# A graph network's layers 1 and 2: one full product per block in place of quarter-array products for two, and a sum over chunks by VectorE ahead of the sum over nodes

## The chip, the cores and the metric

The kernel runs on one core of one Trainium2 chip. The metric is the device time of one execution in microseconds; the time before is the median of three runs.

## What is computed

Four graph layers follow each other over `x` of 8 batches, 2048 nodes and 64 features. Each layer takes a layer norm and a relu of `x` and adds its result to `x`. The two layers that the change touches, and the last one that the sum over nodes belongs to, are these:

```python
# layer 1, three steps: v <- relu([v, A v] W1^T + b1) W2^T + b2
for _ in range(3):
    effects = einsum('nm,bmd->bnd', adj, v)
    h = concatenate([v, effects], -1)
    h = relu(einsum('bnk,dk->bnd', h, W1) + b1)
    v = einsum('bnk,dk->bnd', h, W2) + b2
x = x + v

# layer 2: one aggregation, a scale and bias for each feature, a linear map
h = maximum(layernorm(x), 0)
agg = einsum('ij,bjf->bif', adj, h)
x = x + einsum('bnf,of->bno', (agg*c*w_nl[:,0] + agg*c*w_nl[:,1] + b_nl), w_out) + b_out

# layer 3: attention over adj > 0.5
h = maximum(layernorm(x), 0)
x = x + elu(softmax(where(adj > 0.5, leaky(s1 + s2^T), -9e15)) @ h)
```

No entry of the given `adj` is above 0.5, so the attention of layer 3 is the mean of `h` over all nodes. The kernel computes that mean and, beside it, tests that the adjacency has the form that this path needs; a general path behind it runs only if the test fails.

## The kernel before

The 8 batches are taken as 4 pairs. The 2048 nodes of a pair are 4 blocks of 512, each with 4 chunks of 128 nodes. A block lies either with its nodes on the partitions (128 partitions, 4 chunks, 128 columns: 64 features of each of the two batches) or with its features on them (128 x 512).

The product with the adjacency (`product`, line 250) takes 32 matrix products of 128 x 128 by 512 columns for a block: 16 chunks, each as a high and a low part of the values (`H` and `L`). The `fill` dictionary names functions that are called between these products, after chunk number `m`; that is how small products of other blocks are put into the stream. After it `scaled` (line 240, VectorE) multiplies the result with the row factors.

Layer 1 goes over the pairs, three steps and four blocks. In each block the result of the aggregation (`g`) and the mapped old features (W1v times `gT[nb]`) are added (line 917, VectorE), then ScalarE applies bias and relu (918). The mapping is done by `map_two` (895 to 907) after chunk 10 of blocks 0 and 2, for two blocks at once. W1v stands twice on the diagonal of a 128 x 128 matrix, so `map_two` takes only the two 64 x 64 blocks: for two node blocks and two batches these are four products of 64 x 64 by 512 columns, each in another quarter of the TensorE array. They go into a tile of two PSUM banks (tag `big`), and ScalarE copies the four results back over `gT`. `finish` (873) brings a block back to nodes by four products of 128 columns (`bn`, line 665) and makes the new high and low parts. In the last step `prepare_next` loads the next pair's block, transposes it (`pt`, line 262, tag `tr`), multiplies it (`bn_u`) and splits it. Two small copies of a constant row (`hb<-ivt`, line 681) belong to it.

Layer 2 goes over pairs and blocks. After chunk 5 of a block, `behind` continues the norms in work and finishes the block before (`finish2`): four products `bn`, an add, and the start of its norm. The norm (`norm_stages`) has three stages: mean, difference and square; variance and its power on GpSimd (194); and the scaling on VectorE (197), after which `done` is called with the result. After chunk 15, `sums(g - 2)` (957 to 966) adds the nodes of block g - 2 for layer 3: four products with a matrix of ones, one for each chunk, accumulated in one PSUM bank `pS` (tag `tr`) over the pair's four blocks. After the fourth, `outputs` computes the mean's elu and adds it to all four blocks.

PSUM is full: the tags `mm`, `big` and `tr` have two buffers each, of one, two and one bank. A buffer is given out in turn, and its next user waits until the last reader of its previous one has finished. The order on each engine is made from the program's order by a scheduler that may put an instruction that is ready ahead of one that waits; on the chip each engine then keeps its order.

Of the kernel before, what the change touches and what calls it, by code (L numbers as in the profile page):

```python
# [8 lines left out]
F32 = mybir.dt.float32  # L9
# [5 lines left out]
ALU = mybir.AluOpType  # L15
AX = mybir.AxisListType
# [26 lines left out]
def uniform_path(  # L43
# [30 lines left out]
    nc = tc.nc  # L74
    P = 128
    B, N, C = x.shape
    NP = B // 2
    NCH = N // P
    NB = N // 512
# [6 lines left out]
    psums = [pro.enter_context(tc.tile_pool(name="psump", bufs=1, space=bass.MemoryType.PSUM))]  # L86
# [14 lines left out]
    def bank(tag, name):  # L101
        return psums[-1].tile([P, 512], F32, tag=tag, name=name)
# [11 lines left out]
    ones = consts.tile([P, P], F32, name="ones")  # L114
# [19 lines left out]
    def nodes(acc):  # L134

        return acc.rearrange("p j f -> p (j f)").rearrange("p (e j c) -> p j e c", e=2, c=C)

    def load_x(layer, p, nb, queue=nc.sync):
        acc = block("acc", f"acc_{layer}_{p}_{nb}", 2)
        fill_x(acc, layer, p, nb, queue)  # L140
        return acc
# [11 lines left out]
    def load_crow(nb, name, tag="crow"):  # L153
        t = work.tile([P, 512], F32, tag=tag, name=f"crow_{name}", bufs=2)
        nc.sync.dma_start(t, crowD[:, nb * 512:(nb + 1) * 512].to_broadcast([P, 512]))
        return t
# [4 lines left out]
    def split(t):  # L161
        return t.rearrange("p j (b c) -> p j b c", b=2)
# [11 lines left out]
    def norm_stages(xt, name, done, out_):  # L174

        z = block("z", f"z_{name}", 3)
        g = groups(z)
        mean = small.tile([P, 8], F32, name="mean")
        nc.vector.tensor_reduce(each(mean), nodes(xt), axis=AX.X, op=ALU.add)
        nc.vector.tensor_scalar(mean, mean, 1.0 / C, None, op0=ALU.mult)  # L180
        firsts.append(nc.vector.tensor_tensor(  # L181
            split(z), nodes(xt), each(mean)[:, :, :, None].to_broadcast([P, 4, 2, C]),
            op=ALU.subtract
        ))
        sq = block("sq", f"sq_{name}", 1)
        squares.append(nc.scalar.activation(sq, z, AF.Square))  # L186
        yield
        var = small.tile([P, 8], F32, name="var", bufs=3)
        nc.vector.tensor_reduce(var, groups(sq), axis=AX.X, op=ALU.add)  # L189
        variances.append(  # L190
            nc.vector.tensor_scalar(var, var, 1.0 / C, EPS, op0=ALU.mult, op1=ALU.add)  # L191
        )
        rstd = small.tile([P, 8], F32, name="rstd", bufs=3)
        powers.append(nc.gpsimd.tensor_tensor(rstd, var, mhalf, op=ALU.pow))  # L194
        yield
        h = z if out_ is None else out_
        scales.append(nc.vector.scalar_tensor_tensor(  # L197
            groups(h), g, 0.0, rstd[:, :, None].to_broadcast([P, 8, C]), op0=ALU.max, op1=ALU.mult
        ))
        done(h)  # L200
        yield

    def norm_relu(xt, name, done, out_=None):
        n = norm_stages(xt, name, done, out_)
        next(n)
        pending.append([n, 2])
# [16 lines left out]
    lastp = []  # L223
# [52 lines left out]
    def term(k, name):  # L276
        pool = l0t if k == 1 else l0f[0]
        return pool.tile([P, 512], F32, tag=f"t{k}", name=name, bufs=(2, 4, 1)[k])
# [286 lines left out]
    nm = "0_1_3a"  # L565
    tx = work.tile([P, 512], F32, tag="z", name=f"t1T_{nm}", bufs=3)
    ps = bank("b1", f"bv_{nm}")
    for m in range(NCH):
        if m in (2, 7, 12):
            go_back(1 + m // 5)  # L570
        for i in range(2):
            nc.tensor.matmul(
                ps, hls[1][m // 4][i][:, m % 4, :], BT[:, m, 3 * 512:],
                start=(m == 0 and i == 0), stop=(m == NCH - 1 and i == 1),
# [80 lines left out]
    def feat(i, name):  # L655

        if i == 0:
            return term(1, name)
        return lastp[0].tile([P, 512], F32, tag="fm", name=name, bufs=4)

    def back_to_nodes(fT, wmat, name, tag="big"):

        ps = psums[-1].tile([P, 4, 2 * C], F32, tag=tag, name=f"bn_{name}")
        for t in range(4):
            nc.tensor.matmul(ps[:, t, :], fT[:, t * P:(t + 1) * P], wmat, start=True, stop=True)  # L665
        return ps
# [63 lines left out]
    def feat_0(p, q):  # L730
        h = load_h(p, q, f"f0_{p}_{q}", l0q)
        return to_feat(h, term(0, f"t0T_{p}_{q}"), f"0_{p}_{q}")

    first_t0 = []
    for p in range(NP):
# [47 lines left out]
        for nb in range(NB):  # L783
            nm = f"0_{p}_{nb}b"
# [3 lines left out]
                fill={12: lambda: first_t0.append(feat_0(0, 0))} if p + nb == 0 else {},  # L788
                tag="mm" if p + nb else "b0",
# [32 lines left out]
    w1vT, w1eT, w2T, wos, w1v2, w1e2, r1e, rbo = (wl[:, i, :] for i in range(8))  # L822
# [46 lines left out]
    def layer1(n, p):  # L869
        hl, gT = ops[n]  # L870
        steps = 3
        for s in range(steps):
            last = s == steps - 1
            g_new, hl_new = [], []

            def finish(nb):
                nm = f"1_{p}_{s}_{nb}"
                if last:
                    acc = load_x(1, p, nb)
                    pn = back_to_nodes(g_new[nb], w2T, nm)  # L880
                    nc.vector.tensor_tensor(nodes(acc), split(pn), nodes(acc), op=ALU.add)
                    keep(p, nb, acc, f"2_{p}_{nb}", rows4(rbo))
                else:
                    pn = back_to_nodes(g_new[nb], w1e2, nm)
                    nc.vector.tensor_tensor(split(pn), split(pn), rows4(r1e), op=ALU.add)
                    hl_new.append(halves(pn, nm))

            def mid():
                if last:
                    prepare_next(n + 1, 2)  # L890
                else:
                    finish(2)

            def map_two(nb):

                ph = psums[-1].tile([P, 2, 512], F32, tag="big", name=f"ph_1_{p}_{s}_{nb}")
                w = w1v2 if s else w1vT
                two = (slice(0, C), slice(C, P))
                for i in range(2):
                    for bb in range(2):  # L900
                        nc.tensor.matmul(  # L901
                            ph[two[bb ^ i], bb, :], w[two[bb], two[bb]], gT[nb + i][two[bb], :],
                            start=True, stop=True,
                        )
                for i in range(2):
                    for bb in range(2):
                        nc.scalar.copy(gT[nb + i][two[bb], :], ph[two[bb ^ i], bb, :])  # L907

            for nb in range(NB):
                nm = f"1_{p}_{s}_{nb}"  # L910
                crow = load_crow(nb, nm)
                g = feat((s + 1) % 2, f"g_{nm}")
                fill = {8: mid} if nb == 3 else {}
                if nb % 2 == 0:
                    fill[10] = lambda: map_two(nb)
                product(hl, nb, nm, g, crow, fill=fill)
                gadd = nc.vector.tensor_tensor(g, g, gT[nb], op=ALU.add)
                nc.scalar.activation(g, g, AF.Relu, bias=b1s if s else b1c)
                g_new.append(g)
                go_on()  # L920
                if nb in (1, 2):
                    finish(nb - 1)
                    if last:
                        prepare_next(n + 1, nb - 1)
                if s < 2:
                    k = 2 * (8 * p + 4 * s + nb)
                    with tc.issue_after(gadd.ins):
                        test(k)
                        test(k + 1)
            if last:  # L930
                finish(2)
                prepare_next(n + 1, 3)
            if last and n == NP - 1:

                put_off.append(lambda: finish(3))
            else:
                finish(3)
            gT, hl = g_new, hl_new
# [5 lines left out]
    accs, es, zs, pS = [], [], {}, {}  # L944

    def finish2(g):
        p, nb = divmod(g, NB)
        nm = f"acc_2_{p}_{nb}"
        acc = term(1, nm) if p % 2 else feat(1, nm)
        acc = acc.rearrange("p (j f) -> p j f", j=4)  # L950
        accs.append(acc)
        fill_x(acc, 2, p, nb)
        pn = back_to_nodes(es[g], wos, f"2_{p}_{nb}")
        nc.vector.tensor_tensor(nodes(acc), split(pn), nodes(acc), op=ALU.add)
        norm_relu(acc, f"3_{p}_{nb}", lambda h: zs.update({g: h}))

    def sums(g):
        p, nb = divmod(g, NB)
        if nb == 0:
            pS[p] = bank("tr", f"pS_{p}")  # L960
        for t in range(4):
            nc.tensor.matmul(  # L962
                pS[p][:, :2 * C], ones, zs[g][:, t, :],
                start=(nb == 0 and t == 0), stop=(nb == NB - 1 and t == 3),
            )
        if nb == NB - 1:
            outputs(p)
# [649 lines left out]
```

## Time and profile before

| | us |
|---|---|
| median of the runs (1238.1 to 1239.29) | 1239.18 |
| the profiled execution | 1238.1 |
| its span, first to last instruction | 1236.1 |
| products of layers 1 and 2 with the adjacency, H and L (line 250, 1024 each) | 409.7 and 401.3 busy |
| `ph` (line 901, 64*64, 192 records) | 26.1 busy |
| `pS` (line 962, 128 records) | 18.0 busy |
| copies of `map_two` (line 907, ScalarE, 96) | 55.8 busy |

Layer 1 runs from about 628 us to 1064, layer 2 from there to the end. A fp32 product appears as two records in the profile, so the 64 products of `sums` are 128. Busy times of products overlap, since they are pipelined: a record of 512 columns lasts 0.39 us, while the next one begins 0.23 us after it. What a product costs is therefore read from the starts of its neighbours, not from its own duration.

### The profile page before, as it was taken

The numbers are of one execution on the slowest core, as the hardware profiler recorded it, in microseconds if no ns is written. First come the engines' busy times: TensorE is split into PE (matmuls) and PEld (weight loads), VectorE is DVE, ScalarE is ACT, GpSimd is POOL, SyncE is SP. The second block draws the span as 40 slices with busy tenths as digits, with TensorE's granted clock in tenths as the row PEclk, the third lists the DMA queues.
The fourth block names the chain that finished last, engine by engine and source line by source line (L and its number), as shares of the span: only waits on it lengthen the run. The fifth ranks groups of instructions, "written<-read, shape, count | busy, mean of one in ns | idle before, by whom it ended". The sixth has DMA issues, their size and how long they took to land.

```text
span 1236.1 us, 15662 instructions
## 1 busy us (share of the span) xinstructions
PE 1197.7 (97%) x5798; PEld 843.7 (68%) x5798; DVE 744.7 (60%) x1940; ACT 237.0 (19%) x377; POOL 223.5 (18%) x233
## 2 busy tenths in 40 slices
PE   5899999999999999999989999999999999999995
PEld 4675555555675557655557787787877877888884
DVE  5456888777757774477654436444644545566664
ACT  6610001000010000000022233233223223211100
POOL 5410222211131111011110013003101400331211
PEclk9999999999999999999999999999999999999997
DMA  9951334332332233122256526543743563533311
GB/s 355 379 154 47 102 105 115 84 86 77 90 102 73 64 82 85 54 64 64 60 128 126 134 85 156 132 85 123 158 115 92 154 131 92 155 124 112 119 58 40
DMA packets 100985, 140.99 MB, mean 114 GB/s; under 512 B 43772, under 2 KB 58108, under 8 KB 98852
## 3 DMA queue, kind: packets, MB, share of 16 engines
q1 hardware_dynamic: 82820, 80.74, 24.9%
q0 software_dynamic: 11776, 48.15, 12.9%
q10 hardware_dynamic: 6304, 11.01, 2.8%
q8 instruction: 48, 0.79, 0.3%
q14 instruction: 37, 0.30, 0.1%
HBM read 95.03 MB, written 35.66 MB: 106 GB/s over the span
## 4 chain that ended last, share of the span: by engine, by line
PE 92%; DMA 3%; DVE 3%; issue 1%; POOL 1%; ACT 0%; SPq 0%; POOLq 0%; ACTq 0%
PE bv L250 38%; PE y L711 26%; PE bn L665 5%; PE bv_1b L250 2%; PE bv_3b L250 2%; PE bv_2b L250 2%; PE bv_0b L250 2%; PE ph L901 2%; DMA BT<-in_adj_dram 2%; PE bn_u L665 1%; PE bv_0a L250 1%; PE bv_3a L250 1%; PE pt L262 1%; PE bv_2a L250 1%; PE pS L962 1%; PE bv_1a L250 1%
## 5 line engine op out<-in xcount | busy, mean ns | idle before, releaser
L250 PE MATMUL bv<-BT,H 128*128 128x512 f32 x1024 | 409.7, 400 | 0.0
L250 PE MATMUL bv<-BT,L 128*128 128x512 f32 x1024 | 401.3, 392 | 0.0
L250 PEld LDWEIGHTS bv<-BT,H 128*128 128x128 f32 x1024 | 193.0, 188 | 56.6 <-issue 19.5
L250 PEld LDWEIGHTS bv<-BT,L 128*128 128x128 f32 x1024 | 193.0, 188 | 37.0
L720 DVE SCALAR_TENSOR_TENSOR acc<-y,emb,acc 128x128 f32<-128x128 f32 x512 | 176.3, 344 | 65.7 <-PE y L711 65.7
L720 DVE SCALAR_TENSOR_TENSOR odd<-y,emb,odd 128x128 f32<-128x128 f32 x448 | 153.4, 343 | 0.0
L711 PE MATMUL y<-wt,t0T 64*128 64x512 f32 x512 | 143.7, 607 | 2.4 <-DVE odd L720 1.7
L194 POOL TENSOR_TENSOR rstd<-var,mhalf 128x8 f32<-128x8 f32 x64 | 105.7, 1653 | 182.4 <-DVE var L191 181.0
L240 DVE TENSOR_TENSOR g<-bv,crow 128x512 f32<-128x512 f32 x48 | 33.2, 691 | 173.0 <-PE bv L250 173.0
L186 ACT ACTIVATE sq<-z 128x512 f32<-128x512 f32 x64 | 40.4, 631 | 398.0 <-DVE z L181 388.1
L711 PEld LDWEIGHTS y<-wt,t0T 64*128 64x128 f32 x512 | 45.8, 185 | 63.3 <-issue 57.1
L692 POOL TENSOR_TENSOR acc<-acc,b2r 128x512 f32<-128x512 f32 x16 | 22.2, 1389 | 315.7 <-DVE z L181 315.7
L692 POOL TENSOR_TENSOR acc<-acc,wl 128x512 f32<-128x512 f32 x16 | 20.5, 1283 | 295.8 <-DVE z L181 295.8
L711 PE MATMUL y<-wt,t1T 64*128 64x512 f32 x256 | 66.7, 589 | 0.0
L197 DVE SCALAR_TENSOR_TENSOR z<-z,rstd 128x512 f32<-128x512 f32 x64 | 44.7, 703 | 35.2 <-POOL rstd L194 35.2
L665 PEld LDWEIGHTS bn<-wl,g 128*128 128x128 f32 x384 | 49.8, 193 | 7.5 <-issue 3.0
L665 PE MATMUL bn<-wl,g 128*128 128x128 f32 x384 | 51.5, 277 | 2.6 <-issue 2.6
L189 DVE TENSOR_REDUCE var<-sq 128x8 f32<-128x512 f32 x64 | 43.6, 681 | 15.6 <-ACT sq L186 15.6
L846 DVE SCALAR_TENSOR_TENSOR junk<-mt,cols,st 128x512 uint8<-128x512 bf16 x64 | 47.7, 745 | 2.7 <-DMA mt<-MD 2.3
L907 ACT COPY g<-ph 64x512 f32<-64x512 f32 x64 | 37.2, 581 | 49.6 <-PE ph L901 48.8
L711 PEld LDWEIGHTS y<-wt,t1T 64*128 64x128 f32 x256 | 27.1, 187 | 27.8 <-issue 27.8
L181 DVE TENSOR_TENSOR z<-acc,mean 128x512 f32<-128x512 f32 x56 | 38.3, 692 | 6.0 <-DMA hs<-z 4.6
(213 smaller groups left out, 1649.7 us busy)
## 6 DMA issues: line engine op xcount, KB each, us to landing
BT<-in_adj_dram POOLq DMA_DIRECT2D x16, 1024.0 KB, 19.6
crow<-crowD SPq DMA_DIRECT2D x64, 256.0 KB, 3.4
st<-in_adj_dram SPq DMA_DIRECT2D x64, 256.0 KB, 3.5
hs<-z POOLq DMA_DIRECT2D x40, 256.0 KB, 3.1
xs<-acc POOLq DMA_DIRECT2D x32, 256.0 KB, 2.4
MD<-BT POOLq DMA_DIRECT2D x16, 512.0 KB, 5.6
acc<-xs SPq DMA_DIRECT2D x32, 256.0 KB, 3.9
hb<-hs SPq DMA_DIRECT2D x28, 256.0 KB, 3.5
```

What stands on the lines that cost most here:

```text
L181: firsts.append(nc.vector.tensor_tensor(split(z), nodes(xt), each(mean)[:, :, :, None].to_broadcast([P, 4, 2, C]), op=ALU.subtract))
L186: squares.append(nc.scalar.activation(sq, z, AF.Square))
L189: nc.vector.tensor_reduce(var, groups(sq), axis=AX.X, op=ALU.add)
L194: powers.append(nc.gpsimd.tensor_tensor(rstd, var, mhalf, op=ALU.pow))
L197: scales.append(nc.vector.scalar_tensor_tensor(groups(h), g, 0.0, rstd[:, :, None].to_broadcast([P, 8, C]), op0=ALU.max, op1=ALU.mult))
L250: nc.tensor.matmul(ps, hl[m // 4][i][:, m % 4, :], BT[:, m, nb * 512:(nb + 1) * 512], start=(m == 0 and i == 0), stop=(m == NCH - 1 and i ...
L665: nc.tensor.matmul(ps[:, t, :], fT[:, t * P:(t + 1) * P], wmat, start=True, stop=True)
L692: nc.gpsimd.tensor_tensor(nodes(acc), nodes(acc), more, op=ALU.add)
L711: nc.tensor.matmul(y[:, bb, :], terms[k][hs_, ts], wt[hs_, k, dg * 512:(dg + 1) * 512], start=(k == 0), stop=(k == K - 1),)
L720: last = nc.vector.scalar_tensor_tensor(xj, yd, ec, old, op0=ALU.mult, op1=ALU.add)
L846: nc.vector.scalar_tensor_tensor(junk, mt, cols[:, i, :], st, op0=ALU.mult, op1=ALU.not_equal, accum_out=bad[:, i, q:q + 1],)
L907: nc.scalar.copy(gT[nb + i][two[bb], :], ph[two[bb ^ i], bb, :])
```

## The change

In layer 1 `map_two` and its copies go. Each block has one full product of the 128 x 128 matrix with `gT[nb]`, after chunk 12, into a bank `ph` of the tag `tr`, and the add takes it from there.

In layer 2 `done` of the norm calls `add_chunks`. For all blocks but the last of the kernel, VectorE adds the four chunks into a tile `hs4` of 128 x 128, and `sums` multiplies that alone with the ones. The last block keeps its four products.

```diff
-            def map_two(nb):
-                ph = psums[-1].tile([P, 2, 512], F32, tag="big", name=f"ph_1_{p}_{s}_{nb}")
-                w = w1v2 if s else w1vT
-                two = (slice(0, C), slice(C, P))
-                for i in range(2):
-                    for bb in range(2):
-                        nc.tensor.matmul(
-                            ph[two[bb ^ i], bb, :], w[two[bb], two[bb]], gT[nb + i][two[bb], :],
-                            start=True, stop=True,
-                        )
-                for i in range(2):
-                    for bb in range(2):
-                        nc.scalar.copy(gT[nb + i][two[bb], :], ph[two[bb ^ i], bb, :])
-
             for nb in range(NB):
                 nm = f"1_{p}_{s}_{nb}"
                 crow = load_crow(nb, nm)
+                ph = bank("tr", f"ph_{nm}")
                 g = feat((s + 1) % 2, f"g_{nm}")
                 fill = {8: mid} if nb == 3 else {}
-                if nb % 2 == 0:
-                    fill[10] = lambda: map_two(nb)
+                fill[12] = lambda: nc.tensor.matmul(
+                    ph, w1v2 if s else w1vT, gT[nb], start=True, stop=True
+                )
                 product(hl, nb, nm, g, crow, fill=fill)
-                gadd = nc.vector.tensor_tensor(g, g, gT[nb], op=ALU.add)
+                gadd = nc.vector.tensor_tensor(g, ph, g, op=ALU.add)
...
-        norm_relu(acc, f"3_{p}_{nb}", lambda h: zs.update({g: h}))
+        norm_relu(acc, f"3_{p}_{nb}", lambda h: add_chunks(g, h))
+
+    def add_chunks(g, h):
+        zs[g] = [h[:, t, :] for t in range(4)]
+        if g + 1 < NP * NB:
+            hs4 = lastp[0].tile([P, 2 * C], F32, name="hs4", bufs=2)
+            nc.vector.tensor_reduce(hs4, h.rearrange("p t f -> p f t"), axis=AX.X, op=ALU.add)
+            zs[g] = [hs4]
...
-        for t in range(4):
+        for t, z in enumerate(zs[g]):
             nc.tensor.matmul(
-                pS[p][:, :2 * C], ones, zs[g][:, t, :],
-                start=(nb == 0 and t == 0), stop=(nb == NB - 1 and t == 3),
+                pS[p][:, :2 * C], ones, z,
+                start=(nb == 0 and t == 0), stop=(nb == NB - 1 and t == len(zs[g]) - 1),
             )
```

## The prediction, made before the changed kernel was run

> **What bounds the kernel now.** I read the page's head first, then who waits on TensorE in the stages of layers 1 and 2 (from 628 us on), then TensorE's timeline around the products that change, then the last 20 us of all engines.
>
> From the page:
>
> ```profile
> span 1236.1 us, 15662 instructions
> PE 1197.7 (97%) x5798; PEld 843.7 (68%) x5798; DVE 744.7 (60%) x1940; ACT 237.0 (19%) x377; POOL 223.5 (18%) x233
> PEclk9999999999999999999999999999999999999997
> ```
>
> TensorE is busy 97% of the span at full clock. The waits of TensorE from 628 us to the end:
>
> ```profile
> PE pS L962 <- DVE z L197: 5.3, 1, 5.3
> PE bn L665 <- issue: 2.6, 1, 2.6
> PE bn_u L665 <- ACT gT L267: 0.7, 1, 0.7
> ```
>
> In 608 us there are three waits: one in the tail (5.3), one in the first step of layer 1 (2.6), one of 0.7. Everything else is TensorE's own rate, so a product added or removed in these layers counts in full, and work on VectorE or ScalarE only where it makes TensorE wait. So I need three prices: the quarter-array group `ph` of now, the full `ph` that comes, and the group `pS`.
>
> *Price of `map_two`.* A step of layer 1 without waits (from one `ph` to the next of its kind) is this row of the windows:
>
> ```profile
> 785.53:820.75 35.22, 35.22 (x181) 27.78 (x183) 16.42 (x32) 9.66 (x16) 0.00 (x0) 1.00 0.55 120
> ```
>
> It holds 4 block products of 32, 2 calls of `map_two` and 4 groups `bn`. The timeline paces undisturbed products at 0.2267 us (24 of them from 755.26 to 760.70), so 128 take 29.02. A group of four 128-column products costs 0.908: a block of layer 2 repeats every 9.07 us (1106.68 to 1115.76) and has 32 products (7.25) and two such groups, `bn` and `pS`. Then 35.22 - 29.02 - 4 x 0.908 leaves 2.57, or 1.28 for each `map_two`. The timeline of TensorE shows the same at one place:
>
> ```profile
> 785.14 0.39 PE L250 MATMUL bv<-BT,L 128*128 128x512 f32 x1
> 785.46 1.09 PE L901 MATMUL ph<-g,wl 64*64 64x512 f32 x8
> 786.48 0.19 PEld L250 LDWEIGHTS bv<-BT,H 128*128 128x128 f32 x1 [0.81 <-issue]
> 786.48 0.50 PE L250 MATMUL bv<-BT,H 128*128 128x512 f32 x1
> 786.82 0.39 PE L250 MATMUL bv<-BT,L 128*128 128x512 f32 x1
> 787.05 0.40 PE L250 MATMUL bv<-BT,H 128*128 128x512 f32 x1
> ```
>
> From the last product ahead to the third behind is 1.91; three paces of 0.2267 taken off leave 1.23, and the next ten run at 0.23, which makes up the rest. The eight records (each fp32 product has two) lie in one stretch of 1.09: the four quarters do run beside each other. The gap ahead is 0.32 instead of 0.23.
>
> *Price of a full fp32 product of 512 columns amid such a stream.* The kernel has one kind, the bias product `pb`:
>
> ```profile
> 61.60 0.40 PE L479 MATMUL bv_2a<-BT,L 128*128 128x512 f32 x1
> 61.83 1.02 PE L406 MATMUL pb<-bd,embT 128*128 128x512 f32 x2
> 62.28 0.80 PE L479 MATMUL bv_0a<-BT,H 128*128 128x512 f32 x1
> 62.92 0.40 PE L479 MATMUL bv_1a<-BT,H 128*128 128x512 f32 x1
> ...
> 63.38 0.40 PE L479 MATMUL bv_3a<-BT,H 128*128 128x512 f32 x1
> 63.63 1.12 PE L406 MATMUL pb<-bd,embT 128*128 128x512 f32 x2
> 64.19 0.79 PE L479 MATMUL bv_0a<-BT,L 128*128 128x512 f32 x1
> 64.83 0.39 PE L479 MATMUL bv_1a<-BT,L 128*128 128x512 f32 x1
> ```
>
> From 61.60 to 62.92 lie one `pb` and two paces of that stretch (0.233): 1.32 - 0.47 = 0.85. The second: 1.45 - 0.47 = 0.98.
>
> **What the Trainium skill says.** "TensorEngine Tiling (Array Packing)", Key Properties: tiles execute in parallel, but a change of tiling mode drains the engine. The trace agrees: four quarters in 1.09 us, and the wider gap ahead of them; this is the part that a full product does not pay. "FP8 and Floating Point Precision", TensorE Precision Notes: true FP32 takes four passes. Agrees: 0.85 for 512 columns is 3.8 paces of the single-pass stream (0.2267). "VectorE: DVE Perf Modes", the tier table: fp32 `tensor_tensor` has one rate, with or without a PSUM operand, and `tensor_reduce` one rate too. The trace agrees: L917 from SBUF 690 ns, L881 from PSUM 683, reduce L179 685.
>
> **The change part by part.**
>
> 1. *Layer 1, `map_two` goes.* It runs 4 pairs x 3 steps x 2 times, 24 x 1.28 = 30.7 us of TensorE, all on the path.
>
> 2. *Layer 1, one full `ph` for each block comes.* 48 of them. I take 0.88: the first `pb` (0.85, nothing odd around it) and 0.03 for the slightly slower pace that follows every fp32 group in this stream. Sum 42.2. Parts 1 and 2: +11.5. Ends: 0.85 gives +10.1, 0.98 gives +16.3. So the full array does in two products what the quarters did beside each other in 1.28; only the drain is saved.
>
> 3. *ScalarE loses its 96 copies* (L907, 581 ns, 55.8 us). They ran while TensorE went on, and ScalarE is busy 19%: nothing on the path.
>
> 4. *The add reads `ph` from PSUM* instead of SBUF: 683 against 690 ns, nothing. It waits for `ph` as well, which ends some six products before `bv`.
>
> 5. *The `tr` banks.* `ph` takes one of the two `tr` buffers from the third quarter of its block until the add. Behind it in the ring come the transposes `pt` of the third-step `prepare_next`. The one after the last block takes the buffer of that block's `ph`, so it must wait for the add. At the end of the second pair that add ends at 855.44, while the `pt` now starts at 854.24: 1.2 us later. TensorE has products of the next pair ready (ten of them already lie between `pt` and `bn_u`), and `L` of the last block is ready at 859.23 while its use comes about 862.2, so I cost it at nothing. If the order kept TensorE standing at `pt`, it would be 1.2 us in each of three pairs.
>
> 6. *The wait in the first step.* `bn` at 647.77 waits 2.6 us for the relu, and that stands on ScalarE behind a copy of `ivt` (646.75) that waits for a load. By then two new `ph` and one old group less put TensorE 2 x 0.88 - 1.28 = 0.5 later; the load is not moved by that, so the wait shrinks: -0.5.
>
> 7. *Layer 2, one `pS` product instead of four, blocks 0 to 14.* Four cost 0.908, that is 8 records at 0.1106 and 0.02 around them. Two records: 0.24; with a little for a short product among long ones I take 0.26 (ends 0.24 and 0.40). Each saves 0.65. The sums of blocks 0 to 12 lie before the last `bn` that the tail hangs on (block 14's, at 1210.1): 13 x 0.65 = -8.4 (ends -6.6 and -8.7). That of block 13 lies behind it and only makes TensorE wait for VectorE; that of block 14 lies in TensorE's wait of 5.3.
>
> 8. *VectorE's reduce*, 15 times. Nearest row 685 ns; the strided read might cost more, and I bound it by twice that, below by 0.6. A block of layer 2 has 5.8 us of VectorE in 9.07 (75.9 busy in the 117.8 us from 1088.7 to 1206.5), and the block shrinks to 8.42, and `sums` comes some 5 us behind `z`: hidden, except at the end. There the timeline shows VectorE without a gap:
>
> ```profile
> 1217.02 0.69 DVE L197 SCALAR_TENSOR_TENSOR z<-z,rstd 128x512 f32<-128x512 f32 x1 [0.56 <-POOL rstd L194]
> 1217.71 0.69 DVE L954 TENSOR_TENSOR acc<-bn,acc 128x512 f32<-128x512 f32 x1
> 1217.77 0.97 PEld L962 LDWEIGHTS pS<-z,ones 128*128 128x128 f32 x8 [0.29 <-DVE z L197]
> ```
>
> The reduce of block 14 comes between these first two, and the last norm starts 0.7 later: +0.7 (ends 0 if it is put into a later gap, +1.4).
>
> Sum: +11.5 - 0.5 - 8.4 + 0.7 = +3.3 us. The profiled execution took 1238.1 (its span 1236.1 and 2.0 around it), so 1241.4; the median of the runs is 1.1 above it, which gives 1242.5.
>
> **Rivals.**
>
> *A, not slower: the first wait goes.* The order on ScalarE is set anew, and without `map_two`'s copies (ended at 637.9) the `ivt` copy may fall behind the relus instead of ahead. Then 2.6 of wait go, of which 0.5 is counted, and with it the slow stretch behind it: `bn` 1.39 against 0.8 and six products 2.57 against 1.36, 1.8 in all. That is 3.9 more, 1238.6. It decides from the point where the relu of block 0 stands ahead of that copy. Against it: the copy stood far ahead of its data already, and nothing here moves the load. 0.16.
>
> *B: the full `ph` costs 0.98*, as the second `pb` did: 48 x 0.10 = 4.8 more, 1247.3. Against it: that `pb` is one of two, and its weights waited 0.3 us. 0.10.
>
> *C: TensorE stands at `pt`* (part 5), 3 x 1.2 = 3.6 more, 1246.1. For it: ring order demands the wait. Against it: the order already has products of the next pair ahead of waiting ones. 0.09.
>
> That the change might not do what it says I leave out: in layer 1 the weights are block-diagonal, so one full product covers both batches, and in layer 2 the column sums of four added chunks are those of the block.
>
> **How the numbers follow.** The main case has 0.65, its own range 1240 to 1245. With the bounds of parts 2, 7 and 8 and the rivals the range is 1238.5 to 1247.5. A measurement of this kernel tells 0.2%, 2.5 us, from no change. Main case: 0.17 within it, 0.48 slower. A: 0.04 faster, 0.12 within. B and C: slower. Together 0.04, 0.29, 0.67.
>
> **What would show it.** Right: a step of layer 1 takes about 36.2 us instead of 35.22 (2.57 off, 4 x 0.88 on), a block of layer 2 about 8.42 instead of 9.07, TensorE stays gapless, one reduce of 0.7 ahead of the last `acc`. Wrong: `ph` pieces that cost 1.0 or more (B), `pt` with idle time (C), no wait in the first step (A), a block of layer 2 at 9.0, where the short product would not be cheaper.

## The result, and the profile after

The changed kernel takes 1244.68 us in the median (1244.5 to 1245.27, 4 runs), the kernel before beside it 1239.24. The ratio is 1.0042, interval 1.0025 to 1.006: 5.4 us slower, where 3.3 were predicted. The time lies in the predicted range (1238.5 to 1247.5), but two terms of the sum are wrong, and they offset each other. The page of the changed kernel:

```profile
span 1243.5 us, 15171 instructions
PE 1203.4 (97%) x5612; PEld 850.1 (68%) x5612; DVE 758.4 (61%) x1955; ACT 181.6 (15%) x281; POOL 223.8 (18%) x233
```

TensorE is as full as before, with 186 fewer records; ScalarE has lost its 96 copies. The profiled pair differs by 7.4 us of span, more than the medians do, since the one before was the fastest of its runs and this one the slowest. Who waits on TensorE from 628 us on (total, times, longest), in the changed kernel:

```profile
PE pS L957 <- DVE z L197: 5.6, 1, 5.6
PE bn L665 <- DVE e L240: 4.4, 4, 1.9
PE pS L957 <- DVE hs L949: 1.4, 1, 1.4
PE bn_u L665 <- ACT gT L267: 0.7, 1, 0.7
```

The wait of 2.6 us in layer 1's first step is gone, and a new one has come in layer 2: four times TensorE stands before `bn` until VectorE has made `e`. Cut by the starts of TensorE's groups in the two timelines, the 7.4 us lie as follows.

| stretch | before | after | difference |
|---|---|---|---|
| up to the first product of layer 1 | 629.1 | 628.7 | -0.4 |
| layer 1, to the first product of layer 2 | 443.9 | 451.9 | +8.0 |
| layer 2, to `bn` of the last block | 143.5 | 141.7 | -1.8 |
| from there to the end | 19.6 | 21.2 | +1.6 |

*Layer 1.* Two steps in a row, as windows of the changed kernel (limits; length; busy of TensorE, of its weight loads, of VectorE, ScalarE and GpSimd; then the granted clock, the DMA share and GB/s):

```profile
750.31:786.60 36.29, 36.29 (x170) 29.04 (x169) 19.35 (x39) 5.65 (x9) 5.13 (x6) 1.00 0.61 159
786.60:822.88 36.28, 36.28 (x169) 29.04 (x169) 16.41 (x32) 5.02 (x8) 0.00 (x0) 1.00 0.58 117
```

A step has no gap and takes 1.07 us more than the 35.22 of before: 12.8 in twelve steps. What takes 4.4 of that back is seen on ScalarE in the first step. First the timeline of the kernel before, then that of the changed one:

```profile
646.75 0.30 ACT L681 COPY hb<-ivt 1x128 f32<-1x128 f32 x1 [8.83 <-DMA acc<-xs]
646.96 1.33 ACT L918 ACTIVATE g<-g,b1c 128x512 f32<-128x512 f32 x2
```

```profile
639.11 0.72 ACT L905 ACTIVATE g<-g,b1c 128x512 f32<-128x512 f32 x1 [5.84 <-DVE var L191]
645.98 0.30 ACT L681 COPY hb<-ivt 1x128 f32<-1x128 f32 x1 [6.15 <-DMA hb<-hs]
647.23 0.72 ACT L905 ACTIVATE g<-g,b1c 128x512 f32<-128x512 f32 x1 [0.95 <-DVE g L904]
```

Before, the relus of blocks 0 and 1 stood behind a copy that waited for a load. Now block 0's relu stands ahead of that copy, at 639.1, and its `bn` starts at 645.1 without a wait. With the wait of 2.6 went the slow products behind it, 1.8.

*Layer 2.* A block without a wait takes 8.43 us instead of 9.07, as it should. But of 14 such savings, 9.0 us, only 1.8 arrive. VectorE's timeline in the block with the longest interior wait (start, length, operation, idle time before it and what ended it), in the changed kernel:

```profile
1145.06 0.69 DVE L197 SCALAR_TENSOR_TENSOR z<-z,rstd 128x512 f32<-128x512 f32 x1 [1.81 <-POOL rstd L194]
1145.79 1.07 DVE L949 TENSOR_REDUCE hs<-z 128x128 f32<-128x512 f32 x1
1146.78 0.68 DVE L232 TENSOR_TENSOR L<-hb,H 128x512 fp32r<-128x512 f32 x1
1147.38 0.68 DVE L941 TENSOR_TENSOR acc<-bn,acc 128x512 f32<-128x512 f32 x1
...
1151.64 0.69 DVE L232 TENSOR_TENSOR L<-hb,H 128x512 fp32r<-128x512 f32 x1 [1.45 <-ACT H L230]
1152.25 0.68 DVE L189 TENSOR_REDUCE var<-sq 128x8 f32<-128x512 f32 x1
1152.96 0.17 DVE L191 TENSOR_SCALAR var<-var 128x8 f32<-128x8 f32 x1
1153.04 0.69 DVE L240 TENSOR_TENSOR e<-bv,crow 128x512 f32<-128x512 f32 x1
```

The same stretch, same pair and block, before:

```profile
1136.37 0.69 DVE L197 SCALAR_TENSOR_TENSOR z<-z,rstd 128x512 f32<-128x512 f32 x1 [1.21 <-POOL rstd L194]
1137.25 0.69 DVE L232 TENSOR_TENSOR L<-hb,H 128x512 fp32r<-128x512 f32 x1 [0.19 <-ACT H L230]
1138.62 0.69 DVE L954 TENSOR_TENSOR acc<-bn,acc 128x512 f32<-128x512 f32 x1 [0.68 <-PE bn L665]
```

The reduce takes 1.07 us, not 0.69, and lies ahead of everything that follows in its queue. Behind it: `acc`, which begins the next norm; and `L`, whose end frees the buffer for the next load of `hb`. That load leaves at 1147.49, when `L` ends, and `H` on ScalarE waits for it (first line: start and duration of the load, from the chain that ended last):

```profile
1147.49 3.42 DMA hb<-hs
1150.98 0.62 ACT L230 CAST H<-hb 128x512 fp32r<-128x512 f32 x1 [5.25 <-DMA hb<-hs]
1151.51 0.63 ACT L186 ACTIVATE sq<-z 128x512 f32<-128x512 f32 x1
```

The next `L` on VectorE waits for this `H`. Behind `L` stands `var`, which needs `sq`, and behind `var` stands `e`, done at 1153.7. The products for `e` had ended at 1152.0. On TensorE:

```profile
1153.79 1.39 PE L665 MATMUL bn<-wl,e 128*128 128x128 f32 x8 [1.83 <-DVE e L240]
1154.82 0.77 PE L250 MATMUL bv<-BT,H 128*128 128x512 f32 x1
1155.40 0.63 PE L250 MATMUL bv<-BT,L 128*128 128x512 f32 x1
1155.82 0.63 PE L250 MATMUL bv<-BT,H 128*128 128x512 f32 x1
```

After 1.83 us of wait the next six products begin at 0.43 us from each other instead of 0.23. That block takes 10.16 us instead of 8.43. So 7.1 of the saving are lost (14 x 0.64 = 8.96 saved, 1.82 arrived): 4.4 in the four waits, 1.7 in the slow products, the rest in small pieces. One of the fourteen savings, block 13's, the prediction had not counted itself.

How near the limit this was can be read from VectorE's own waits in layer 2 of the kernel before:

```profile
DVE acc L954 <- PE bn L665: 15.4, 10, 2.6
```

VectorE stood before `acc` until TensorE had made `bn`, in ten of the sixteen blocks, and not evenly: from the block whose `acc` starts at 1130.6 on, four blocks in a row wait 0, 0.7, 1.3 and 2.6 us, the next four 0, 0.7, 2.1 and 2.6. That is 4.5 to 5.3 for four blocks, 1.1 to 1.3 a block: the slack. A faster block takes 0.64 of it and the reduce 1.06, together 1.7: in the changed kernel this wait has shrunk to 0.9 in all, and TensorE waits instead. The reduce's own reader is not what waits: no `pS` before the tail stands for `hs`.

### The profile page after: what moved, and what is told of

Read it like the earlier page. It is cut to its first block, busy times and chain, and to the rows that moved or that the text cites. A ratio compares the mean times of both kernels' runs of the same rounds, so it can differ in the third digit from the quotient of the medians.

```text
span 1243.5 us, 15171 instructions
## 1 busy us (share of the span) xinstructions
PE 1203.4 (97%) x5612; PEld 850.1 (68%) x5612; DVE 758.4 (61%) x1955; ACT 181.6 (15%) x281; POOL 223.8 (18%) x233
## 4 chain that ended last, share of the span: by engine, by line
PE 86%; DVE 6%; DMA 3%; POOL 2%; issue 1%; ACT 1%; POOLq 0%; ACTq 0%; DVEq 0%
PE bv L250 33%; PE y L711 26%; PE bn L665 4%; PE ph L900 3%; DMA BT<-in_adj_dram 3%; PE bv_3b L250 2%; PE bv_2b L250 2%; PE bv_1b L250 2%; PE bv_0b L250 2%; POOL rstd L194 1%; PE bn_u L665 1%; PE bv_0a L250 1%; PE bv_3a L250 1%; PE pt L262 1%; PE bv_2a L250 1%
## 5 line engine op out<-in xcount | busy, mean ns | idle before, releaser
L250 PE MATMUL bv<-BT,H 128*128 128x512 f32 x1024 | 427.5, 417 | 0.0
L250 PEld LDWEIGHTS bv<-BT,L 128*128 128x128 f32 x1024 | 193.3, 189 | 47.9 <-issue 11.5
L905 ACT ACTIVATE g<-g,b1s 128x512 f32<-128x512 f32 x32 | 23.2, 724 | 137.1 <-DVE g L904 137.1
L691 POOL DMA_DIRECT2D hs<-z x32 | 18.6, 582 | 133.5 <-DVE z L197 96.9
```

The source lines that it names most:

```text
L250: nc.tensor.matmul(ps, hl[m // 4][i][:, m % 4, :], BT[:, m, nb * 512:(nb + 1) * 512], start=(m == 0 and i == 0), stop=(m == NCH - 1 and i ...
```

## The experiments

All differences in us are the ratio's share of the median of the kernel before on the same chip (1238.4 to 1238.9); for the kernels with one execution they are plain differences to that median. Each half of the change was run alone, with the other half as before; the edit is then the one half of the diff shown above.

**Layer 1 alone.**

> The change of layer 1 alone, layer 2 as before. Theory 1 (what the two traces suggest): a step of layer 1 takes 1.07 us more, 12.8 us in twelve steps, and the wait of 2.6 us in the first step with the slow products behind it (together 4.4) is gone, because the relu of block 0 now stands ahead of the copy of ivt on ScalarE: 8.4 us slower than before. Rival (as predicted: the wait only shrinks by 0.5): 11 to 12 us slower, with a wait of about 2 us at the first bn.

1246.01 us, ratio 1.0063 (1.0049 to 1.0078), 7.8 us slower (6.1 to 9.7), where theory 1 had 8.4 and the rival 11 to 12. Theory 1 holds: `bn` of block 0 at 646.5 does not wait.

**Layer 2 alone.**

> The change of layer 2 alone, layer 1 as before (quarter-array products). Theory 1: as in the changed kernel, new waits of TensorE for e and for the sum over chunks eat most of what the short sums save: within 2 us of before. Rival (as predicted: all but the last block's reduce is hidden): 7 to 8 us faster, and the waits seen in the changed kernel come from the shifted start of layer 2, not from the reduce.

1236.14 us, ratio 0.998 (0.9973 to 0.9987), 2.5 us faster, a little more than theory 1's 2. The rival, which is the prediction's figure, falls: with layer 1 as before the waits are there too, so they do not come from the shifted start. TensorE's waits in layer 2:

```profile
PE bn L665 <- DVE e L240: 4.1, 5, 2.0
PE pS L970 <- DVE hs L962: 1.8, 1, 1.8
```

The halves add: +7.8 - 2.5 = +5.3, where the whole change measured +5.4. In the traces, from the first product of layer 1 to the end, they are +7.8 and -1.9, and the whole change is +7.8: the long wait with the slow products behind it is not in the trace of layer 2 alone, where no wait before the tail is longer than 0.9. These are single executions, and the medians do not show that difference.

**Layer 2 without the reduce.** This edit and the two further edits of the reduce are shown against the kernel with layer 2 changed alone.

```diff
-            nc.vector.tensor_reduce(hs4, h.rearrange("p t f -> p f t"), axis=AX.X, op=ALU.add)
-            zs[g] = [hs4]
+            zs[g] = [h[:, 0, :]]
```

> As the kernel with the change of layer 2 alone, but the reduce is left out and the sum over nodes takes the first chunk only, so three quarters of the nodes are missing from the mean. Theory 1 (the reduce's 1.06 us on VectorE delays what stands behind it there: the low parts, so the next load, so e): 8 to 9 us faster than before, blocks of layer 2 at 8.43 us without waits. Rival 2 (TensorE, being faster, runs into the loads and the norm chain whatever VectorE does): 2 to 4 us faster, the waits for e remain.

1230.72 us, ratio 0.993 (0.9915 to 0.9945), 8.7 us faster. From the second block to the last but one each takes 8.44 us, and `e` is waited for once, at the end:

```profile
PE bn L665 <- DVE e L240: 0.6, 1, 0.6
```

From block 0's `bn` to block 14's it takes 8.2 us less than before (4.7 less with the reduce), and from there to the end 26.0, as before (29.0 with the reduce). So TensorE's saving was there to be had, and it was the reduce that took it.

**The reduce replaced.** GpSimd adds in two steps; then VectorE in two plain adds.

```diff
-            nc.vector.tensor_reduce(hs4, h.rearrange("p t f -> p f t"), axis=AX.X, op=ALU.add)
+            nc.gpsimd.tensor_tensor(h[:, 0:2, :], h[:, 0:2, :], h[:, 2:4, :], op=ALU.add)
+            nc.gpsimd.tensor_tensor(hs4, h[:, 0, :], h[:, 1, :], op=ALU.add)
```

> The change of layer 2 alone, but GpSimd adds the chunks (two adds, of 256 and of 128 columns) in place of VectorE's reduce. Theory 1 (the reduce's place on VectorE is what costs): as without the reduce, 7 to 8 us faster than before, blocks of 8.43 us without waits for e; GpSimd's adds take about 1 us and lie between two rstd. Rival (adds on GpSimd slow VectorE or delay rstd): 2 to 4 us faster, waits remain.

1230.78 us, ratio 0.9942 (0.9927 to 0.9956), 7.2 us faster, with 0.8 us of waits for `e`. The adds take 0.74 and 0.46 us on GpSimd (medians; the first at most 1.07). Theory 1 holds.

> The change of layer 2 alone, but VectorE adds the chunks by two plain adds of 256 and 128 columns in place of one reduce over a strided view. Theory 1: the two adds take about 0.7 us together instead of 1.06, and the chain behind them comes 0.35 us earlier: 3 to 5 us faster than before. If the reduce's own 1.06 us were not what counts: as with the reduce, 2 us faster.

1231.45 us, ratio 0.994 (0.9925 to 0.9955), 7.4 us faster: more than expected, as much as with GpSimd. The groups of VectorE in this kernel (busy, mean ns, idle before) are

```profile
L962 DVE TENSOR_TENSOR z<-z 128x256 f32<-128x256 f32 x15 | 6.3, 422 | 0.3
L963 DVE TENSOR_TENSOR hs<-z 128x128 f32<-128x128 f32 x15 | 4.3, 290 | 0.3
```

0.71 us instead of 1.06. A difference of 0.35 us in a block is worth 5 us in the kernel. This agrees with the slack of 1.1 to 1.3 us above: 0.64 + 0.71 = 1.35 just uses it up (VectorE's wait before `acc` is down to 0.9 in all here too, but `e` is not late until the end), and 1.7 goes beyond it. No run varies the slack itself.

**The reduce over neighbours.** Is it the stride or the number of results that makes it long?

```diff
-            nc.vector.tensor_reduce(hs4, h.rearrange("p t f -> p f t"), axis=AX.X, op=ALU.add)
+            nc.vector.tensor_reduce(hs4, h.rearrange("p t f -> p (t f)").rearrange("p (f t) -> p f t", t=4), axis=AX.X, op=ALU.add)
```

> The change of layer 2 alone, with the reduce taken over four neighbouring columns instead of the same column of four chunks, so the 128 sums are of other entries than the mean needs. Theory 1 (the strided read makes the reduce 1.06 us instead of the 0.69 of the other reduces): about 0.69 us and 3 to 5 us faster than before. Rival (128 results instead of 8 make it long): still about 1.06 us and within 3 us of before.

One execution, 1230.68 us against 1238.46, 7.8 us faster: more than the 3 to 5 expected, as with the two adds. The group in this kernel, and below it that of the kernel with layer 2 changed alone:

```profile
L962 DVE TENSOR_REDUCE hs<-z 128x128 f32<-128x512 f32 x15 | 10.2, 682 | 0.3
```

```profile
L962 DVE TENSOR_REDUCE hs<-z 128x128 f32<-128x512 f32 x15 | 16.0, 1064 | 0.3
```

The same reduce with the same 128 results takes 682 ns over neighbours and 1064 over elements 512 bytes apart. The stride is the cause. The Trainium skill has a reason for it, in "SBUF — State Buffer", the note on cachelines under the section on the DMA port swizzle: each access that crosses to a new 16-byte line pays. No run here tells that reason from another cost of the stride. The prediction had bounded the strided read without it.

**The two prices of layer 1.** The mapping was left out of both kernels.

```diff
-                if nb % 2 == 0:
-                    fill[10] = lambda: map_two(nb)
```

> The kernel before without map_two: the mapped old features are left out, the unmapped ones are added. It prices map_two: a step of layer 1 takes 35.22 - 2 x 1.28 = 32.65 us. With the wait in the first step gone too (the relu stands ahead of the copy of ivt in this one), about 35 us faster than before; about 31 if the wait stays.

1204.33 us, one execution, 34.6 under the kernel before beside it, and no wait in the first step: the relu of block 0 (639.4) stands ahead of the copy of `ivt` (647.8) here too, so taking `map_two` and its copies out is enough to change that order.

> The changed kernel without the full product ph: the unmapped old features are added. It prices ph: a step takes 36.29 - 4 x 0.91 = 32.65 us, as in the kernel before without its mapping, 43.7 us less than the changed kernel over twelve steps. If ph cost more by what it displaces than by itself, the step would be shorter than 32.65 or waits would vanish.

1203.75 us, one execution. From the first product of layer 1 to the first `bn` of layer 2's own blocks it takes 419.1 us where the changed kernel takes 462.0: 42.9 less, where 43.7 were expected. Windows of one step, in the kernel before and then in the changed one, both without the mapping:

```profile
748.32:781.02 32.70, 32.70 (x161) 27.52 (x160) 17.54 (x34) 5.14 (x8) 1.14 (x2) 1.00 0.69 158
```

```profile
749.72:782.42 32.70, 32.70 (x161) 27.53 (x160) 17.53 (x34) 5.13 (x8) 1.14 (x2) 1.00 0.70 163
```

The steps are equal, so `map_two` costs (35.22 - 32.70) / 2 = 1.26 us and a full `ph` (36.29 - 32.70) / 4 = 0.90. Its place in the stream shows most of it: one `ph` and two paces of 0.2267 lie between 642.62 and 643.94 in the changed kernel, which leaves 0.87; the rest is the slower pace behind it.

```profile
642.62 0.39 PE L250 MATMUL bv<-BT,L 128*128 128x512 f32 x1
642.85 1.02 PE L900 MATMUL ph<-gT,wl 128*128 128x512 f32 x2
643.30 0.80 PE L250 MATMUL bv<-BT,H 128*128 128x512 f32 x1
643.94 0.40 PE L250 MATMUL bv<-BT,L 128*128 128x512 f32 x1
```

**The wait in the first step.** In the kernel before, one order changed:

```diff
+    relus = []
...
-                nc.scalar.copy(h[0:1, 0, :], ivt)
+                with tc.issue_after(relus[-1].ins) if relus else nullcontext():
+                    nc.scalar.copy(h[0:1, 0, :], ivt)
...
-                nc.scalar.activation(g, g, AF.Relu, bias=b1s if s else b1c)
+                relus.append(nc.scalar.activation(g, g, AF.Relu, bias=b1s if s else b1c))
```

> The kernel before with one order changed: the copy of ivt into the next pair's block may be issued only behind the relu that precedes it in the program. Theory 1 (the wait in the first step is the relu standing behind that copy on ScalarE): 4 to 5 us faster than before, no wait of TensorE in the first step. Rival 3 (another wait takes its place, since the load or the norm behind the copy comes later): no change, within 1 us.

1235.4 us, ratio 0.9977 (0.9967 to 0.9986), 2.8 us faster (1.7 to 4.1). The wait is gone, so the order was its cause and rival 3 falls; the size is below the 4 to 5 expected. From the first product of layer 1 to the first of layer 2 it takes 440.4 instead of 443.9, 3.5 less. One new wait has come, 0.4 us at a `pt` that now stands behind the copy; the rest of the difference stays open.

**Both gains together.** Layer 1 of before with this order, layer 2 with the two adds for all blocks but the last two, whose sums lie in TensorE's wait at the end.

> Layer 1 with the quarter-array products of before, the copy of ivt behind the relu, and layer 2 with the chunks added by GpSimd for all blocks but the last two. If the two gains lie on different stretches of TensorE's path they add: 3 us from the first step and 7 to 8 from layer 2, 10 to 11 us faster than before. Rival (the copy moved back delays the next pair's norm or load and takes part of it away): 7 to 8 us.

1227.49 us, ratio 0.9909 (0.9892 to 0.9926): 11.3 us faster than before.

> The same with VectorE's two plain adds in place of GpSimd's: 10 to 11 us faster than before if the gains add, and not slower than with GpSimd, since the adds of 0.7 us fitted without waits when layer 2 was changed alone.

1228.59 us, ratio 0.9912 (0.9896 to 0.9928): 10.9 us faster. The gains add within the noise (2.8 and 7.2 or 7.4 alone; leaving block 14's adds out, which is new here, may have a part in the rest, and no run separates it), and the two ways to add the chunks cannot be told apart. Both versions beat both kernels, and both leave out the layer 1 part of the change.

## Why the prediction was right, and where it was wrong

- *Parts 1 and 2 were right.* `map_two` 1.26 instead of 1.28, `ph` 0.90 instead of 0.88: +12.8 us instead of +11.5. The `pb` of before served as the price of a product that the kernel did not yet have. That two full products cost more than four quarters beside each other was the main term.
- *Part 3 was right for TensorE and still misjudged.* The copies lay on no path, but taking them off ScalarE let its order be made anew. Rival A named just this, with its price, and it happened; the prediction gave it 0.16. It had even written why the copy would stay, and no view of the profile showed the scheduler's choice.
- *Parts 4 and 5 were right.* L904 takes 691 ns from PSUM, and no `pt` waits in the changed kernel. Rival C did not come, nor did B.
- *Part 6 was mis-sized by rival A's 3.9:* the wait did not shrink by 0.5, it and its slow products went, 4.4 in the traces. Removed alone, it measured 2.8.
- *Part 7 was right* in its price: 0.64 saved for each block instead of 0.65.
- *Part 8 failed:* "hidden, except at the end". The reduce was bounded at twice the nearest row, but that bound was only applied to the tail. In the middle there were two tests. That `sums` comes well behind `z` held: `pS` does not wait for `hs` before the tail. Busy time against block length, 5.8 of 9.07, was the wrong test for an engine that works in a chain with others: the slack stood in VectorE's wait before `acc`, 1.1 to 1.3 us a block, and was not read. Up to `bn` of block 14, where the prediction had -8.4, only -3.1 us arrived; without the reduce it was -8.2.
- *The tail, also part 8,* cost 3.0 instead of 0.7. The prediction counted it from `bn` of block 14; from there to the end it is 26.0 us before and 29.0 after. (The table above starts one block later, so part of this stands there among the waits.) First the `acc` behind that `bn` in the kernel before, then in the changed one, where it begins 3.1 us after `bn` instead of 1.1, behind a late `z` and the reduce of block 13:

```profile
1211.21 0.69 DVE L954 TENSOR_TENSOR acc<-bn,acc 128x512 f32<-128x512 f32 x1 [1.56 <-PE bn L665]
```

```profile
1215.91 0.69 DVE L197 SCALAR_TENSOR_TENSOR z<-z,rstd 128x512 f32<-128x512 f32 x1 [1.81 <-POOL rstd L194]
1216.64 1.07 DVE L949 TENSOR_REDUCE hs<-z 128x128 f32<-128x512 f32 x1
1217.63 0.68 DVE L941 TENSOR_TENSOR acc<-bn,acc 128x512 f32<-128x512 f32 x1
```

That is 2.0. The other 1.0 is the reduce of block 14, the one that was priced at 0.7; it stands ahead of the last `acc`:

```profile
1223.42 0.69 DVE L197 SCALAR_TENSOR_TENSOR z<-z,rstd 128x512 f32<-128x512 f32 x1 [1.21 <-POOL rstd L194]
1224.15 1.02 DVE L949 TENSOR_REDUCE hs<-z 128x128 f32<-128x512 f32 x1
1225.09 0.68 DVE L941 TENSOR_TENSOR acc<-bn,acc 128x512 f32<-128x512 f32 x1
```

Cut as the prediction cut it, the two traces differ by +8.0 in layer 1, where it had +11.0; by -3.1 up to `bn` of block 14, where it had -8.4; and by +3.0 behind it, where it had +0.7. That is +7.8, and -0.4 ahead of layer 1, where nothing was changed (the traces of all kernels here put the start of layer 1 between 628.7 and 632.4), makes the 7.4 of the profiled pair. So a gain of 3.0 that was not in the sum stood against losses of 5.3 and 2.3 that were not in it either. The direction rests on parts 1 and 2, which were right; that 3.3 came out as near to 5.4 as it did is luck.

## What to carry to other kernels

When work moves from a full engine to a half-empty one, do not compare busy time with the span: look at how long the receiving engine waits for the full one at the point of the loop where they meet, take off what the full engine will save, and see whether the new work fits into the rest. Take the mean over a few turns of the loop, not over the turns that wait. In this kernel the account agrees with three lengths of the added work (0.68 and 0.71 us fitted, 1.06 did not); it was not tried on another. Small products that run beside each other in quarters of the array are paid together (here 1.26 us for two blocks); one full product per block in their place pays for every block (0.90 each). When instructions are removed, read again what stands behind which wait in each queue, for the order may change, and a gain from that belongs to the order and can be had alone.

## What the runs showed of the hardware

A `tensor_reduce` of 512 fp32 elements to 128 results took 682 ns over neighbours and 1064 ns over elements 512 bytes apart. After TensorE had waited 1.83 us its next six products began 0.43 us apart instead of 0.23, and the clock granted to TensorE from 1155.4 to 1157.9 was 0.50, against 1.00 from 1158.2 on. The wait of 2.6 us in the kernel before was followed by the same (0.43 us apart, granted clock 0.50 from 649.7 to 651.4). After waits of 0.37 (at 1108.7 in the changed kernel) and 0.92 (at 1146.3 with layer 2 changed alone) the products stayed 0.23 apart and the clock was 1.00. The Trainium skill, "TensorE: Matmul & The Clock Gate", the section "What's actually happening", has the half-rate state begin after at least one idle window of about 3.4 us; here waits of 1.83 and 2.6 us were enough.
